# A planned two-block transformer kernel: searched issue order, later gate loads, constant rows on ScalarE

## Chip, cores, metric

One core of one Trainium2 chip. The metric is the device time of one execution in microseconds; the figure for a kernel is the median of its runs.

## What is computed

Two transformer blocks follow one another on x (32 x 128 x 256). The first is conditioned through shift, scale and gate vectors, which a product of the conditioning vector and `ada_w` gives; the second through scales and shifts of its normalisations.

```python
# first block
xm1 = _ln(x) * (1 + scale_sa) + shift_sa
x = x + gate_sa * (self_attention(xm1) @ sa_proj_w + sa_proj_b)
x = x + (cross_attention(_ln(x), context) @ ca_proj_w + ca_proj_b)
xm3 = _ln(x) * (1 + scale_ff) + shift_ff
x = x + gate_ff * (gelu(xm3 @ fc1_w + fc1_b) @ fc2_w + fc2_b)
# second block
x = x + rope_self_attention(_adaln(x, 1)) @ sa_out_w.T
x = x + rope_cross_attention(_adaln(x, 2), context) @ ca_out_w.T
x = x + gelu(_adaln(x, 3) @ ffn_w1.T + ffn_b1) @ ffn_w2.T + ffn_b2
```

All is float32, with 16 heads of 16 and a hidden width of 1024. Only the first block has gates: one row of 256 numbers for each batch entry and gate, multiplied into the output of a projection.

## The kernel before

The batch of 32 is cut into 16 groups of two (256 rows). Eight streams (`NS`) each carry one group through a block and then take the next. A group passes in the first block through normalisation, self-attention, normalisation, cross-attention, normalisation and feed-forward, then goes to memory (`middle`); later it comes back for the second block.

**The planner.** Each stream is a Python generator. Before every step it yields four things: when its inputs are ready, the engine, the kinds of buffer it needs, and a rank. `Clock` holds a model of the engines' free times and of the buffers (`clock.slots`), with a cost written beside each step (`clock.use("pe", 0.86 * n)`). `Tasks.run` takes for each engine the waiting task with the lowest lateness, rank and turn among those that could start within 0.02 us of the earliest, and then issues the engine whose choice starts first. The instructions are so issued in the planner's order; each engine, and the DMA queue of SP, works its own list in that order. What the model leaves out shows as a wait on the chip.

**Buffers.** There are one `scores` tile (four banks), one `small`, three `products` tiles in PSUM; five sets of `heads` (queries, keys, values, `top`); three `ou`; one pair of `ht` for feed-forward; and four `y` tiles. A `y` has two uses: `normed_T` writes normalised rows into it (L532), which TensorE transposes (L544), and `load_gate` loads gate rows into it from memory (L866), broadcast over 128 partitions, 256 KB.

**Attention** (from L695): for each half, scores (L708), their maxima on VectorE (`top`, L720), a transpose of those (L733), queries less maxima (`qa`, L737), scores again, the exponential on ScalarE (L746), the product with values (L754), and a copy to `ou` (L760). When both halves are copied, `over_sums` moves sums and rows by DMA: `few` (L772), `xt` (L774), a reciprocal (L777), `inv` (L780, L785), and the multiplication (L788) that the projection L821 waits for.

**The gates before.** `first_block` loads the self-attention gate right after the keys' product, before attention, and the stream loads the feed-forward gate before `fed_forward` starts. `project` multiplies gate and bias on GpSimd (L811), adds that to x (L812), multiplies the product in PSUM by the gate on VectorE (L830, into the gate's own tile) and adds it to x on GpSimd (L834), which frees the tile.

**Setting up.** `set_up` writes constant rows into queries and keys of each head set, on VectorE for the first (L338) and on GpSimd for the others in pieces of 256 (L335), then clears values and `top` (L341, L344). `the_rest` computes the modulations, gates and folded biases; `modulation`, `gated` and `with_values` put matrix products and the VectorE steps that read them into one planner's step.

Of the kernel before, what the change touches and what calls it, by code (L numbers as in the profile page):

```python
# [30 lines left out]
NEVER = 1e9  # L31


class Clock:


# [4 lines left out]
    def __init__(self):  # L41
        self.free = dict.fromkeys(("pe", "dve", "act", "pool", "sp", "none"), 0.0)
        many = {"sc": 1, "at": 1, "mm": 3, "pt": 2, "set": NA, "qa": 2, "ou": 3, "st": 2, "ht": 1,
                "y": 4, "cx": 3, "x": NS + 1}
        self.slots = {kind: [0.0] * n for kind, n in many.items()}
        self.table, self.way = None, "full"
        self.now = 0.0
        self.landed = 2.0
# [57 lines left out]
def when(t):  # L106
    return t() if callable(t) else t
# [6 lines left out]
class Tasks:  # L114


    def __init__(self, clock):
        self.clock = clock
        self.waiting = []

    def spawn(self, gen, owner):

        self.step([gen, None, owner])

    def step(self, task):
        task[1] = next(task[0], None)
# [3 lines left out]
    def run(self):  # L130
        clock = self.clock
        while self.waiting:

            first, chosen = {}, {}
            for task in self.waiting:
                ready, engine, kinds, rank = task[1]
                start, late = max(when(ready), clock.slot(kinds)), 0.0
                if engine in ("exp", "gelu"):
                    late = 0.0 if engine == clock.table else clock.TABLE
                    engine = "act"  # L140
                start = max(start, clock.free[engine])
                first.setdefault(engine, []).append((start, late, rank, task))
            for engine, l in first.items():
                horizon = min(start + late for start, late, _, _ in l)
                l = [(late, rank, task[2].turn(), start, i) for i, (start, late, rank, task) in enumerate(l)
                     if start + late <= horizon + 0.02]
                late, _, _, start, i = min(l)
                chosen[engine] = (start, first[engine][i][3])
            start, task = min(chosen.values(), key=lambda c: c[0])
            assert start < NEVER  # L150
            clock.now = start
            self.waiting.remove(task)
            self.step(task)
# [53 lines left out]
def two_blocks(ctx: ExitStack, tc: tile.TileContext, a: dict, out: bass.AP):  # L207
# [113 lines left out]

    clock.slots["set"] = [NEVER] * NA
    clock.use("pool", 1.5)
    clock.use("dve", 3.0)
    clock.use("act", 4.6)

    def set_up(i):
        hd = heads[i]
        for to, at in ((hd.q, None), (hd.k, 0)):
            src = rows[:, C:C + 1].to_broadcast([P, C]) if at is None else rows[:, 0:C]  # L330
            src = src.unsqueeze(2).to_broadcast([P, C, GT])
            if i:
                for c in range(C):
                    yield 2.5, "pool", "", 4
                    nc.gpsimd.tensor_copy(to[:, c, :], src[:, c, :])  # L335
                    clock.use("pool", 0.43)
            else:
                nc.vector.tensor_copy(to, src)  # L338
                clock.use("dve", 1.2)
        yield 0.0, "pool", "", 4  # L340
        nc.gpsimd.memset(hd.v, 1.0)  # L341
        clock.use("pool", 0.95)
        yield 0.0, "pool", "", 4
        nc.gpsimd.memset(hd.top, 0.0)  # L344
        clock.give("set", i, clock.use("pool", 0.2))

    r_sa, r_ca, r_fc2, r_f2 = [const.tile([P, D], F32, name=f"r_{name}") for name in ("sa", "ca", "fc2", "f2")]
    gbias = {"sa": spare[1][:B, 0:D], "ff": spare[1][:B, D:2 * D]}
# [78 lines left out]
    def landed(name):  # L427
        return lambda: there.get(name, NEVER)

    def modulation(name, w, emb, bias, wcol, bcol, one):  # L430

        slot, ps = mm([P, KC, B])
        t = const.tile([P, KC, B], F32, name=f"mod_{name}")
        for c in range(KC):
            at = wcol + c * P
            for k in range(KC):
                nc.tensor.matmul(
                    ps[:, c, :], lhsT=w[:, k, at:at + P], rhs=embT[emb][:, k, :],
                    start=(k == 0), stop=(k == KC - 1),
                )  # L440
        for c in range(KC):
            b = bias[:, bcol // P + c:bcol // P + c + 1]
            nc.vector.tensor_scalar(t[:, c, :], ps[:, c, :], b, 1.0 if one else 0.0, ALU.add, ALU.add)
        clock.use("pe", 1.0)
        clock.give("mm", slot, clock.use("dve", 0.5))
        return t

    mods, gates, biases = {}, {}, {"fc2": r_fc2, "f2": r_f2}

    def the_first():  # L450
        yield max(t_ada, 6.5), "pe", "mm", 0
        scale = modulation("sa_scale", ada_lo, "silu", c_ada, D, D, True)
        yield 0.0, "pe", "mm", 0
        mods["L0", "sa"] = scale, modulation("sa_shift", ada_lo, "silu", c_ada, 0, 0, False)

    def gated(name, w, wcol):

        slot, ps = mm([B, D])
        for k in range(KC):
            nc.tensor.matmul(ps, lhsT=embT["silu"][:, k, :], rhs=w[:, k, wcol:wcol + D],  # L460
                             start=(k == 0), stop=(k == KC - 1))
        t = gbias[name]
        nc.vector.tensor_tensor(t, ps, t, ALU.add)
        clock.use("pe", 0.9)
        clock.give("mm", slot, clock.use("dve", 0.5))
        gates[name] = dram.tile([B, D], F32, name=f"gate_dram_{name}")
        nc.sync.dma_start(out=gates[name], in_=t)
        clock.dma(2.0)

    def with_values(name, row, bias, w):  # L470

        wide = spare[0][:, 3 * D:4 * D].rearrange("p (k n) -> p k n", k=KC)
        slot, ps = mm([P, D])
        for k in range(KC):
            nc.vector.tensor_copy(wide[:, k, :], bias[:, k:k + 1].to_broadcast([P, P]))
            nc.tensor.matmul(ps, lhsT=wide[:, k, :], rhs=w[:, k, :], start=(k == 0), stop=(k == KC - 1))
        nc.vector.tensor_tensor(row, row, ps, ALU.add)
        clock.use("pe", 0.9)
        clock.give("mm", slot, clock.use("dve", 0.9))

    def the_rest():
        yield landed("gate_sa"), "pe", "mm", 1
        gated("sa", ada_lo, 2 * D)
        yield landed("w_sa"), "pe", "mm", 1
        with_values("sa", r_sa, c_qkv[:, 2 * KC:3 * KC], w_sa.t)
        biases["sa"] = r_sa
        yield landed("w_ca"), "pe", "mm", 1
        with_values("ca", r_ca, c_kv[:, KC:2 * KC], w_ca.t)
        biases["ca"] = r_ca
        yield landed("ff_shift"), "pe", "mm", 2  # L490
        shift = modulation("ff_shift", ada_lo, "silu", c_ada, 3 * D, 3 * D, False)
        yield landed("ada_hi"), "pe", "mm", 2
        mods["L0", "ff"] = (modulation("ff_scale", ada_hi, "silu", c_ada, 0, 4 * D, True), shift)
        yield landed("ada_hi"), "pe", "mm", 2
        gated("ff", ada_hi, D)
        load(lnw[2], "L1_xcond_ln3_w")
        there["ln3"] = clock.load(512)
        for i in (1, 2, 3):
            yield landed(f"ln{i}"), "pe", "mm", 2
            gamma = modulation(f"ln{i}_gamma", lnw[i - 1], "raw", c_ln[i - 1], 0, 0, True)  # L500
            yield landed(f"ln{i}"), "pe", "mm", 2
            mods["L1", i] = gamma, modulation(f"ln{i}_beta", lnw[i - 1], "raw", c_ln[i - 1], D, D, False)
            if i == 2:
                load(w_fc1.t, "L0_xcond_fc1_w")
                w_fc1.there[0] = clock.load(1024)
        load(w_fc2.t, "L0_xcond_fc2_w")
        w_fc2.there[0] = clock.load(1024)
        yield landed("ff_rows"), "none", "", 0
# [330 lines left out]
    def fed_forward(wm, x, t, w1, b1, w2, b2, gate, name):  # L839

        there = Event(FC)
        for f in range(FC):
# [9 lines left out]

            tasks.spawn(gelu(), wm)

        def lhs(k, b):
            return ht[k // (FC // 2)][:, k % (FC // 2), b * S:(b + 1) * S]

# [2 lines left out]
        return t  # L860

    def load_gate(wm, which, g):
        yield (lambda: 0.0 if which in gates else NEVER), "sp", "y", 2
        y = clock.take("y")
        t = ys[y]
        nc.sync.dma_start(out=t, in_=gates[which][g * GB:(g + 1) * GB, :].partition_broadcast(P))  # L866
# [22 lines left out]
    def attended(wm, at, x, masked, t, t_v, w, bias, gate, eps, mod, g, name, then, cx=None):  # L889
# [5 lines left out]
        if masked:  # L895
            end = yield from mask_row(heads[at], zeros, 0)
        clock.give("set", at, when(end))
        t = yield from project(wm, x, lambda k, b: wm.xt[:, k, b * S:(b + 1) * S], KC, w, done, bias, gate, name)
        return (yield from normed_T(wm, x, t, eps, mod, g, then))

# [15 lines left out]
    def first_block(wm, x, t, g):  # L916
# [1 line left out]
        at = yield from take_heads(wm, w_qkv, t)  # L918
        hd = heads[at]
        tk = yield from paired(hd, wm, w_qkv, wm.xt, t)  # L920
        gate = yield from load_gate(wm, "sa", g)
        tv = yield from values(wm, hd, w_qkv, 2 * D, wm.xt, t)
        cx = Context(g)
        t = yield from attended(wm, at, x, False, tk, tv, w_sa, "sa", gate, 1e-6, None, g, n, f"b{g}", cx)
        n = f"b{g}"
        at = yield from take_heads(wm, w_kv, latest(t, cx.there))
        hd = heads[at]
# [28 lines left out]
    def stream(wm, mine, loaded):  # L956

        while loaded:
# [3 lines left out]
                                    f"{'a' if first else 'd'}{g}")  # L962
            t = yield from (first_block if first else second_block)(wm, x, t, g)
            if first:
                gate = yield from load_gate(wm, "ff", g)
                to, args = middle, (w_fc1, c_fc1, w_fc2, "fc2", gate, f"c{g}")
            else:
                to, args = out, (w_fc1, c_f1, w_fc2, "f2", None, f"f{g}")

# [120 lines left out]
```

## Time and profile before

| | us |
|---|---|
| median of three runs | 1525.75 (1525.6 to 1532.34) |
| the profiled execution | 1528.39 |
| its span, first to last instruction | 1526.6 |
| VectorE busy in it | 899.8 |
| ScalarE busy in it | 690.2 |
| GpSimd busy in it | 371.0 |
| mean granted clock of TensorE | 0.985 |

The span leaves 1.8 us of the profiled execution's own time outside. In rows of the profile PE is TensorE's matmuls, PEld its weight loads, DVE VectorE, ACT ScalarE, POOL GpSimd, SP the engine whose queue issues the DMAs (SPq for its sequencer). L12 is line 12 of the kernel. A group's row reads: line, engine, operation, tile written and tiles read, shapes, count, busy time, mean ns of one, then the engine's idle time before such instructions and what ended it.

### The profile page before, as it was taken

The page shows a single profiled execution, that of the slowest core. Times are in us where ns is not written, and L with a number is a line of the kernel's source. Part 1 is how long each engine was busy: PE and PEld are TensorE (multiplying, and loading weights), DVE is VectorE, ACT ScalarE, POOL GpSimd, SP SyncE. Part 2 cuts the span into 40 slices and gives each one's busy share as a digit, 9 for nine tenths or more (in the row PEclk, how much of TensorE's full clock was granted, in tenths as well). Part 3 has the DMA queues.
Part 4 walks back from the last instruction along what each step waited for, and adds up shares of the span by engine and source line. Part 5 has one row for each costly group of instructions (what it writes and reads, how often), then busy time and mean ns, then how long its engine had stood idle before and what let it go on. Part 6 is the DMA issues. An engine that isn't in the chain of part 4 may idle for free.

```text
span 1526.6 us, 39576 instructions
## 1 busy us (share of the span) xinstructions
PE 1449.6 (95%) x16992; PEld 1193.1 (78%) x16992; DVE 899.8 (59%) x1544; ACT 690.2 (45%) x1110; POOL 371.0 (24%) x530
## 2 busy tenths in 40 slices
PE   6998799999999999998999999898999999999998
PEld 4776578888888877887777888776878878887887
DVE  5666555655546565555666564757595666577441
ACT  2443345554555444454534554443335535443541
POOL 6132221223221412334213322212121212222110
PEclk9999799999999999999999999999999999999999
DMA  6422124222222324121331431321131221212110
GB/s 212 143 68 78 60 69 106 70 62 82 80 65 69 89 79 123 54 83 52 91 107 63 132 98 43 95 68 62 53 108 47 76 77 55 95 53 87 33 50 21
DMA packets 107359, 120.50 MB, mean 79 GB/s; under 512 B 11632, under 2 KB 82992, under 8 KB 107184
## 3 DMA queue, kind: packets, MB, share of 16 engines
q1 hardware_dynamic: 107184, 117.98, 25.1%
q8 instruction: 133, 2.18, 0.6%
q14 instruction: 42, 0.34, 0.1%
HBM read 54.92 MB, written 12.68 MB: 44 GB/s over the span
## 4 chain that ended last, share of the span: by engine, by line
PE 77%; DVE 10%; DMA 6%; issue 3%; ACT 2%; SPq 1%; POOL 1%; DVEq 0%; ACTq 0%; POOLq 0%
PE products L583 25%; PE products L821 21%; PE scores L708 15%; PE small L754 6%; PE products L595 5%; DVE top L720 4%; PE products L544 3%; DVE y L532 1%; ACT exp L746 1%; PE small L733 1%; DMA ou<-inv_e 1%; DVE xt L788 1%; DMA ou<-inv_a 1%; DMA inv_a<-few_a 1%; DMA inv_e<-few_e 1%
## 5 line engine op out<-in xcount | busy, mean ns | idle before, releaser
L720 DVE TENSOR_REDUCE top<-scores 128x8 f32<-128x1024 f32 x256 | 300.0, 1213 | 70.2 <-PE scores L708 63.4
L746 ACT ACTIVATE exp<-scores 128x1024 f32<-128x1024 f32 x256 | 248.3, 1023 | 162.5 <-PE scores L708 158.2
L583 PE MATMUL products<-xt,w_ffn_w 128*128 128x256 f32 x1024 | 240.5, 388 | 1.1 <-ACT xt L562 0.9
L821 PE MATMUL products<-w_ffn_w,ht 128*128 128x256 f32 x1024 | 232.2, 382 | 0.0
L583 PEld LDWEIGHTS products<-xt,w_ffn_w 128*128 128x128 f32 x1024 | 191.3, 192 | 34.3 <-issue 2.8
L821 PEld LDWEIGHTS products<-w_ffn_w,ht 128*128 128x128 f32 x1024 | 191.7, 190 | 27.8
L708 PEld LDWEIGHTS scores<-qa,keys 32*128 32x128 f32 x4096 | 129.5, 191 | 66.7 <-issue 21.7
L760 ACT COPY ou<-small 128x512 f32<-128x512 f32 x128 | 75.5, 589 | 233.5 <-PE small L754 231.4
L708 PE MATMUL scores<-qa,keys 32*128 32x128 f32 x4096 | 154.3, 288 | 24.4 <-DVE top L720 12.0
L850 ACT ACTIVATE ht<-products,cols 128x256 f32<-128x256 f32 x256 | 116.5, 474 | 120.1 <-PE products L583 119.2
L708 PEld LDWEIGHTS scores<-keys,queries 32*128 32x128 f32 x4096 | 126.6, 187 | 37.1 <-issue 27.4
L708 PE MATMUL scores<-keys,queries 32*128 32x128 f32 x4096 | 151.2, 284 | 2.6 <-ACT exp L746 1.4
L688 POOL TENSOR_TENSOR st<-st 128x512 f32<-128x512 f32 x64 | 83.2, 1302 | 244.2 <-DVE st L683 224.6
L754 PE MATMUL small<-exp,values 128*32 128x128 f32 x4096 | 140.3, 278 | 1.8 <-ACT ou L760 1.4
L737 DVE TENSOR_TENSOR qa<-queries,small 128x512 f32<-128x512 f32 x128 | 86.3, 674 | 72.5 <-PE small L733 70.5
L583 PE MATMUL products<-xt,w_qkv_w 128*128 128x256 f32 x512 | 126.6, 393 | 1.0 <-ACT xt L562 0.9
L754 PEld LDWEIGHTS small<-exp,values 128*32 128x32 f32 x4096 | 105.3, 110 | 24.5 <-issue 10.1
L826 DVE TENSOR_TENSOR x<-products,x 128x512 f32<-128x512 f32 x64 | 44.1, 689 | 130.3 <-PE products L821 128.4
L788 DVE TENSOR_TENSOR xt<-xt,ou 128x512 f32<-128x512 f32 x64 | 52.7, 824 | 96.1 <-DMA ou<-inv_a 28.4
L583 PEld LDWEIGHTS products<-xt,w_qkv_w 128*128 128x128 f32 x512 | 95.5, 195 | 17.3 <-issue 2.8
L834 POOL TENSOR_TENSOR x<-y,x 128x512 f32<-128x512 f32 x32 | 40.7, 1273 | 277.9 <-DVE y L830 277.9
L603 ACT COPY values<-products 128x512 f32<-128x512 f32 x64 | 40.2, 628 | 132.1 <-PE products L595 129.7
(111 smaller groups left out, 1789.8 us busy)
## 6 DMA issues: line engine op xcount, KB each, us to landing
xt<-ou SPq DMA_DIRECT2D x64, 256.0 KB
keys<-st SPq DMA_DIRECT2D x96, 128.0 KB
queries<-st SPq DMA_DIRECT2D x96, 128.0 KB
cxt<-in_ctx SPq DMA_DIRECT2D x32, 256.0 KB
x<-in_x SPq DMA_DIRECT2D x16, 256.0 KB
y<-gate_dram_sa SPq DMA_DIRECT2D x16, 256.0 KB
keys<-st SPq DMA_DIRECT2D x16, 256.0 KB
ou<-inv_a SPq DMA_DIRECT2D x32, 128.0 KB
```

Of the source, the lines that this page charges most:

```text
L583: nc.tensor.matmul(ps[:, c, :], lhsT=w.t[:, k, at:at + P], rhs=src[:, k, :], start=(k == 0), stop=(k == KC - 1))
L595: nc.tensor.matmul(ps[:, b, :], lhsT=src[:, k, b * S:(b + 1) * S], rhs=w.t[:, k, col:col + D], start=(k == 0), stop=(k == KC - 1))
L688: nc.gpsimd.tensor_tensor(st[:, 0], st[:, 0], st[:, 1], ALU.add)
L708: nc.tensor.matmul(sc[:, r, c * S:(c + 1) * S], lhsT=lhs(slice(32 * r, 32 * r + 32), c), rhs=rhs(slice(32 * r, 32 * r + 32), c), start=Tru ...
L720: nc.vector.tensor_reduce(top[:, r:r + 2, TOP:TOP + 2 * C:2], scs[slot][:, r:r + 2, :].rearrange("p r (c s) -> p r c s", s=S), AX.X, ALU.max)
L737: nc.vector.tensor_tensor(qa, q[:, :, cut], ps.unsqueeze(1).to_broadcast([P, C, S]), ALU.subtract)
L746: nc.scalar.activation(exps[pt][r // 2], scs[slot][:, r:r + 2, :], AF.Exp, scale=SCALE)
L754: nc.tensor.matmul(ats[at][32 * r:32 * r + 32, c * S:(c + 1) * S], lhsT=v[:, b, i:i + HD, :].rearrange("p d t -> p (d t)"), rhs=exps[pt][r ...
L760: nc.scalar.copy(ous[ou[0]][:, :, cut], ats[at].rearrange("p (c s) -> p c s", s=S))
L788: nc.vector.tensor_tensor(wm.xt, wm.xt, by, ALU.mult)
L821: nc.tensor.matmul(ps[:, b, :], lhsT=lhs(k, b), rhs=w.t[:, k, :], start=(k == 0), stop=(k == n - 1))
L850: nc.scalar.activation(ht[f // (FC // 2)][:, f % (FC // 2), :], ps[:, 0, :], AF.Gelu, bias=b1[:, f:f + 1])
```

## The change

It has four parts.

1. A list of 36 numbers, one for each 40 us of the planner's time. Where a number is not zero, it changes the rank of about half the waiting tasks by a hash of the task's number, and sets how far behind the earliest start a task may lie and still be chosen.
2. Gate loads move: the one for self-attention from before attention to after its last product, directly ahead of `project`; the one for feed-forward from before the first hidden product to after the eighth. The planner counts, and the kernel has, three `y` tiles in place of four. A gate load waits in the planner until the gate's rows are in memory.
3. The constant rows of all five head sets are written by ScalarE in ten copies of 128x1024.
4. `modulation`, `gated` and `with_values` are split at the engines' borders; the bias copies of `with_values` come early and into a part of the tile for each; the loads that replace used weights wait for TensorE in the planner.

```diff
+EVERY = 40.0
+ORDER = (
+    200, 7, 0, 0, 0, 0, 297, 0, 0, 0, 0, 0, 0, 0, 0, 0, 129, 264, 0, 0, 0, 312, 0, 0, 0, 388, 0, 0, 109, 188, 182,
+    0, 0, 0, 292, 58
+)
...
-                "y": 4, "cx": 3, "x": NS + 1}
+                "y": 3, "cx": 3, "x": NS + 1}
...
+    def changed(self, task, rank, seed):
+        h = (task[3] * 40503 + seed * 2654435761 >> 4) * 2246822519 >> 11
+        return rank + (0, 0, 0, 0, -2, -1, 1, 2)[h % 8] if seed else rank
...
+            at = int(min(t for e, t in clock.free.items() if e in ("pe", "dve", "act")) / EVERY)
+            seed = ORDER[at] if at < len(ORDER) else 0
+            patience = (0.02, 0.02, 0.3, 0.8)[seed % 4]
...
-                l = [(late, rank, task[2].turn(), start, i) for i, (start, late, rank, task) in enumerate(l)
-                     if start + late <= horizon + 0.02]
+                l = [(late, self.changed(task, rank, seed), task[2].turn(), start, i) for i, (start, late, rank, task) in enumerate(l)
+                     if start + late <= horizon + patience]
...
     def set_up(i):
         hd = heads[i]
-        for to, at in ((hd.q, None), (hd.k, 0)):
...
         yield 0.0, "pool", "", 4
         nc.gpsimd.memset(hd.top, 0.0)
-        clock.give("set", i, clock.use("pool", 0.2))
+        end = clock.use("pool", 0.2)
+        for to, src in ((hd.q, rows[:, C:C + 1].to_broadcast([P, C])), (hd.k, rows[:, 0:C])):
+            yield 2.5, "act", "", 4
+            nc.scalar.copy(to, src.unsqueeze(2).to_broadcast([P, C, GT]))
+            end = max(end, clock.use("act", 1.02))
+        clock.give("set", i, end)
...
-    def modulation(name, w, emb, bias, wcol, bcol, one):
+    def modulation(ready, rank, name, w, emb, bias, wcol, bcol, one):
+        yield ready, "pe", "mm", rank
...
+        yield clock.use("pe", 1.0), "dve", "", 1
         for c in range(KC):
...
-    def with_values(name, row, bias, w):
-        wide = spare[0][:, 3 * D:4 * D].rearrange("p (k n) -> p k n", k=KC)
+    def with_values(ready, name, row, bias, w):
+        yield 8.0, "dve", "", 3
+        wide = spare[0][:, 3 * D:4 * D] if name == "sa" else spare[0][:, 2 * D:3 * D]
+        wide = wide.rearrange("p (k n) -> p k n", k=KC)
+        for k in range(KC):
+            nc.vector.tensor_copy(wide[:, k, :], bias[:, k:k + 1].to_broadcast([P, P]))
+        t = clock.use("dve", 0.4)
+        yield (lambda: max(t, ready())), "pe", "mm", 1
...
             if i == 2:
+                yield clock.free["pe"], "sp", "", 2
                 load(w_fc1.t, "L0_xcond_fc1_w")
...
+        if gate is not None:
+            gate = yield from load_gate(wm, "ff", gate)
...
     def load_gate(wm, which, g):
-        yield (lambda: 0.0 if which in gates else NEVER), "sp", "y", 2
+        yield (lambda: gates_at.get(which, NEVER)), "sp", "y", 2
...
         clock.give("set", at, when(end))
+        if gate is not None:
+            gate = yield from load_gate(wm, gate, g)
         t = yield from project(wm, x, lambda k, b: wm.xt[:, k, b * S:(b + 1) * S], KC, w, done, bias, gate, name)
...
         tk = yield from paired(hd, wm, w_qkv, wm.xt, t)
-        gate = yield from load_gate(wm, "sa", g)
...
-                gate = yield from load_gate(wm, "ff", g)
-                to, args = middle, (w_fc1, c_fc1, w_fc2, "fc2", gate, f"c{g}")
+                to, args = middle, (w_fc1, c_fc1, w_fc2, "fc2", g, f"c{g}")
```

More of the change, by code (lines that the diff above doesn't have):

```diff
@@ L119, in __init__ @@
         self.waiting = []
+        self.spawned = 0
     def spawn(self, gen, owner):
-        self.step([gen, None, owner])
+        self.spawned += 1
+        self.step([gen, None, owner, self.spawned])
+    def changed(self, task, rank, seed):
+        h = (task[3] * 40503 + seed * 2654435761 >> 4) * 2246822519 >> 11
+        return rank + (0, 0, 0, 0, -2, -1, 1, 2)[h % 8] if seed else rank
     def step(self, task):
@@ L323, in two_blocks @@
     clock.use("pool", 1.5)
-    clock.use("dve", 3.0)
-    clock.use("act", 4.6)
+    clock.use("dve", 3.9)
+    clock.use("act", 3.5)
     def set_up(i):
         hd = heads[i]
-        for to, at in ((hd.q, None), (hd.k, 0)):
[L330 to L339, printed above, removed]
         yield 0.0, "pool", "", 4
@@ L443, in modulation, with gated @@
             nc.vector.tensor_scalar(t[:, c, :], ps[:, c, :], b, 1.0 if one else 0.0, ALU.add, ALU.add)
-        clock.use("pe", 1.0)
         clock.give("mm", slot, clock.use("dve", 0.5))
         return t
-    mods, gates, biases = {}, {}, {"fc2": r_fc2, "f2": r_f2}
+    mods, gates, gates_at, biases = {}, {}, {}, {"fc2": r_fc2, "f2": r_f2}
     def the_first():
[L451 to L456, printed above, removed]
+        t = max(t_ada, 6.5)
+        scale = yield from modulation(t, 0, "sa_scale", ada_lo, "silu", c_ada, D, D, True)
+        shift = yield from modulation(t, 0, "sa_shift", ada_lo, "silu", c_ada, 0, 0, False)
+        mods["L0", "sa"] = scale, shift
+    def gated(ready, rank, name, w, wcol):
+        yield ready, "pe", "mm", rank
         slot, ps = mm([B, D])
@@ L461, in gated @@
                              start=(k == 0), stop=(k == KC - 1))
+        yield clock.use("pe", 0.9), "dve", "", 1
         t = gbias[name]
         nc.vector.tensor_tensor(t, ps, t, ALU.add)
-        clock.use("pe", 0.9)
-        clock.give("mm", slot, clock.use("dve", 0.5))
+        end = clock.use("dve", 0.5)
+        clock.give("mm", slot, end)
+        yield end, "sp", "", 1
         gates[name] = dram.tile([B, D], F32, name=f"gate_dram_{name}")
         nc.sync.dma_start(out=gates[name], in_=t)
-        clock.dma(2.0)
@@ L470, in with_values @@
-    def with_values(name, row, bias, w):
-        wide = spare[0][:, 3 * D:4 * D].rearrange("p (k n) -> p k n", k=KC)
+        gates_at[name] = clock.dma(2.0)
+    def with_values(ready, name, row, bias, w):
[6 more added lines that the diff above has]
+        yield (lambda: max(t, ready())), "pe", "mm", 1
@@ L473, in with_values @@
         slot, ps = mm([P, D])
         for k in range(KC):
-            nc.vector.tensor_copy(wide[:, k, :], bias[:, k:k + 1].to_broadcast([P, P]))
             nc.tensor.matmul(ps, lhsT=wide[:, k, :], rhs=w[:, k, :], start=(k == 0), stop=(k == KC - 1))
+        yield clock.use("pe", 0.9), "dve", "", 1
         nc.vector.tensor_tensor(row, row, ps, ALU.add)
-        clock.use("pe", 0.9)
-        clock.give("mm", slot, clock.use("dve", 0.9))
+        clock.give("mm", slot, clock.use("dve", 0.45))
@@ L481, in the_rest @@
+        biases[name] = row
     def the_rest():
[L482 to L495, printed above, removed]
+        yield from gated(landed("gate_sa"), 1, "sa", ada_lo, 2 * D)
+        yield from with_values(landed("w_sa"), "sa", r_sa, c_qkv[:, 2 * KC:3 * KC], w_sa.t)
+        yield from with_values(landed("w_ca"), "ca", r_ca, c_kv[:, KC:2 * KC], w_ca.t)
+        shift = yield from modulation(landed("ff_shift"), 2, "ff_shift", ada_lo, "silu", c_ada, 3 * D, 3 * D, False)
@@ L496, in the_rest @@
+        scale = yield from modulation(landed("ada_hi"), 2, "ff_scale", ada_hi, "silu", c_ada, 0, 4 * D, True)
+        mods["L0", "ff"] = scale, shift
+        yield from gated(landed("ada_hi"), 2, "ff", ada_hi, D)
+        yield clock.free["pe"], "sp", "", 2
         load(lnw[2], "L1_xcond_ln3_w")
@@ L498, in the_rest @@
         for i in (1, 2, 3):
[L499 to L502, printed above, removed]
+            gamma = yield from modulation(landed(f"ln{i}"), 2, f"ln{i}_gamma", lnw[i - 1], "raw", c_ln[i - 1], 0, 0, True)
+            beta = yield from modulation(landed(f"ln{i}"), 2, f"ln{i}_beta", lnw[i - 1], "raw", c_ln[i - 1], D, D, False)
+            mods["L1", i] = gamma, beta
             if i == 2:
+                yield clock.free["pe"], "sp", "", 2
                 load(w_fc1.t, "L0_xcond_fc1_w")
                 w_fc1.there[0] = clock.load(1024)
+        yield clock.free["pe"], "sp", "", 2
         load(w_fc2.t, "L0_xcond_fc2_w")
@@ L920, in first_block @@
         tk = yield from paired(hd, wm, w_qkv, wm.xt, t)
-        gate = yield from load_gate(wm, "sa", g)
         tv = yield from values(wm, hd, w_qkv, 2 * D, wm.xt, t)
         cx = Context(g)
-        t = yield from attended(wm, at, x, False, tk, tv, w_sa, "sa", gate, 1e-6, None, g, n, f"b{g}", cx)
+        t = yield from attended(wm, at, x, False, tk, tv, w_sa, "sa", "sa", 1e-6, None, g, n, f"b{g}", cx)
         n = f"b{g}"
```

## The prediction

> **What bounds the kernel now.** I read the page first, then a table of stretches, then what happens to one tile in the worst stretch.
>
> ```profile
> PE 1449.6 (95%) x16992; PEld 1193.1 (78%) x16992; DVE 899.8 (59%) x1544; ACT 690.2 (45%) x1110; POOL 371.0 (24%) x530
> ...
> PEclk9999799999999999999999999999999999999999
> ...
> PE 77%; DVE 10%; DMA 6%; issue 3%; ACT 2%; SPq 1%; POOL 1%; DVEq 0%; ACTq 0%; POOLq 0%
> ```
>
> TensorE is busy 95% of 1526.6 us and holds 77% of the chain that ended last. The change leaves its 16992 matmuls alone, so only 77.0 us of TensorE idle time and the time at a low clock (mean 0.985) can be won. Where they lie:
>
> ```profile
> 0.00:60.00 60.00, 43.86 (x387) 33.44 (x387) 38.82 (x101) 18.51 (x35) 28.63 (x70) 0.94 0.52 168
> 60.00:108.00 48.00, 46.60 (x569) 38.25 (x568) 30.60 (x53) 21.41 (x37) 13.00 (x18) 1.00 0.35 115
> 108.00:200.00 92.00, 74.10 (x1044) 59.19 (x1044) 48.04 (x70) 36.24 (x53) 17.78 (x25) 0.85 0.21 66
> 200.00:520.00 320.00, 318.25 (x3615) 263.73 (x3614) 180.47 (x317) 168.03 (x278) 84.64 (x123) 1.00 0.27 77
> 520.00:840.00 320.00, 303.53 (x3641) 250.13 (x3639) 192.06 (x324) 145.30 (x234) 92.82 (x125) 1.00 0.28 83
> ...
> 940.00:1120.00 180.00, 165.92 (x2174) 135.19 (x2173) 112.10 (x182) 75.16 (x114) 32.85 (x40) 0.97 0.21 67
> ```
>
> Columns: stretch, its length, busy time of PE, weight loads, DVE, ACT, POOL, granted clock, DMA share, GB/s. Idle PE: 16.1 us before 60, 17.9 in 108 to 200 (clock 0.85), 1.8 in 200 to 520, 16.5 in 520 to 840, 14.1 in 940 to 1120. In the third stretch PE does 74.10 x 0.85 = 63 us of full-clock work in 92: 29 us lost. In its middle one attention chain runs almost alone:
>
> ```profile
> 152.39 2.09 PE L708 MATMUL scores<-qa,keys 32*128 32x128 f32 x32 [2.48 <-DVE top L720]
> 154.41 0.47 PE L733 MATMUL small<-ident,top 128*128 128x128 f32 x1
> 156.59 2.09 PE L708 MATMUL scores<-qa,keys 32*128 32x128 f32 x32 [1.70 <-ACT exp L746]
> ```
>
> Why nothing else was at hand shows in the y tiles, between 95 and 182 us:
>
> ```profile
> L811 POOL TENSOR_TENSOR gb_a<-y,r_sa x8: 729/739/745, 97.9 to 179.6; 128x256 f32<-128x256 f32 x8
> L834 POOL TENSOR_TENSOR x<-y,x x4: 1262/1268/1275, 94.4 to 181.1; 128x512 f32<-128x512 f32 x4
> L866 SPq DMA_DIRECT2D y<-gate_dram_sa x3: 322/326/326, 95.7 to 140.2; - x3
> L830 DVE TENSOR_TENSOR y<-products,y x3: 655/682/691, 131.7 to 179.5; 128x512 f32<-128x512 f32 x3
> ```
>
> All four y tiles serve gates for 87 us: no L532 (normalised rows) and no L544 (their transposes) touches a y. The next normalisation stands at 182.86, and the streams whose projections had ended at 95.6, 133.7 and 140.2 start theirs from 201 on. The kernel starves itself by holding gates.
>
> **Gates behind attention.** 32 gates are held from their load (L866) to the end of L834. The ends sum to 1936 us more than the loads: 60.5 us each, 2.27 tiles of 4 on average until the last ends at 874.7. In the new place a self-attention gate is loaded at the end of attention. The chain from there to the end of L834 took 163.64 to 182.38 = 18.7 us once in the trace. A feed-forward gate is held for landing, what is left of the projection (32 matmuls, 6.91 us), L830 (0.69) and L834 (1.27): some 12. That is 16 x 18.7 + 16 x 12 = 491 us, 0.58 tiles, so three y tiles leave more free (2.4) than four did (1.7). A feed-forward stream that waits for a y now does so with the only ht in its hands, so the next feed-forward waits too; at 0.58 held I cost that at nothing, and without this slack it is the last rival's wait. What is late next is attention itself: it has one scores tile, used 256 times for a product of 1.17 and a reduction or exponential of 1.94 to 2.36, with hops about 3.8: 970 us of 1526, so it is no second wall, though it can bind locally. Bounds for 108 to 200: nothing, or all 29 us. Other streams are ready there, yet the stretch also lacks feed-forward work, whose first product stands at 186.26; I take two thirds: **-19**. 520 to 840 is still the block with gates, and PE waits there are spread over scores, xt and y: bounds 0 and -16.5, I take half, **-8**.
>
> Here a rule can be weighed. The granted clock was 0.50 from 155 to 160 us, while no PE gap between 145 and 200 was over 2.48 us. The Trainium skill (TensorE: Matmul & The Clock Gate, Why this matters for your kernels) asks for no idle gap above about 3 us if the clock is to hold; the trace differs, since here shorter gaps in a row did it. By that rule the 11 us that the low clock cost in 108 to 200 would not come back with the gaps, and the sum would be -24 in place of -31.
>
> **The searched order.** 12 of 36 numbers are not zero. A number changes the ranks of about half the tasks (by -2 to 2) and the patience (0.02, 0.3 or 0.8) in 40 us of the planner's time. Nothing is computed differently; instructions change places on their engines. No row prices this. From both sides: 940 to 1120 lost 14.1 idle and 180 x 0.03 = 5.4 of clock, together at most -19; a foreign order that makes this stretch as poor as 108 to 200 would cost as much. One number (388) covers 1000 to 1040; the planner sees no gate landing and no SP queue, so much of what it gains on paper can be lost: **-5**. The three numbers for 1120 to 1240 lie where only 4.5 us idle are left until the end of the span.
>
> **Constant rows on ScalarE.** POOL drops 32 copies (6.5 + 5.8 = 12.3 us, rows L335), DVE two (0.95 + 0.88). ScalarE gets ten of 128x1024: between 0.95 (DVE's) and 1.18 (twice the 0.589 of a 128x512 ACT copy); near the 1.02 of a 128x1024 exponential, so 10.2 us. ScalarE idled 11.10 us until 14.56, which covers them; without it the first xt is one copy, 1.0 us, late. POOL's last set-up memset (34.1 us) comes to about 7 (five pairs of 0.95 + 0.2 from 1.4), so head sets come free earlier. DVE's bias copies ahead of L476 leave their PE wait (1.45) and the split of modulation lets the first statistics pass the second modulation's wait (1.29 on DVE), part of the 3.19 PE gap at 13.21. Bounds 0 and -9.7 (16.1 less the first load's 6.43): **-3**. Later loads of weights wait in the planner instead of blocking SP (some 29 us of SP waits at L244, none ending a PE wait): 0; PE gets 0 from it whatever SP does next.
>
> **What the gates cost in their new place.** L811 and L812 follow the load at once, so POOL stands until the gate lands, and ve, rstd and st of other streams stand behind it. Before, seven feed-forward gates did so already (32.2 us, up to 7.2); their landing took 3.5 to 4.4 us after issue (185.43 to 188.94, 450.40 to 454.80), and the 40-us stretches with two of them (240 to 280, 440 to 480) show PE busy 40.00 of 40. So nothing on PE from that. On SP the feed-forward load moves past the next x load (256 KB, L301), which no row shows PE waiting for after the start. For self-attention, the 256 KB come ahead of few and xt on SP: the chain few, inv, ou, L788 (about 10 us) gets longer. I take a third of 3.9 = 1.3 us, bounds 0 and 3.9; 16 chains; PE waits of 14.6 us in 12 cases already end at L788, so I let a fifth through: 16 x 1.3 x 0.2 = **+4** (bounds 0 and 62).
>
> **Sum:** -19 - 8 - 5 - 3 + 4 = -31. The profiled execution took 1528.39 (span 1526.6 and 1.8 around it), giving 1497; the median 1525.75 lies 2.6 lower: **1495 us**.
>
> **Rivals.**
> - *A fuller mend.* 29 + 16.5 + 19.5 + 9.7 lost us could come back; four fifths of these 75 are 60: 1466. For it: 200 to 520 runs with 1.8 us idle, so the mix can fill PE. Against: the first feed-forward product cannot come at once. 0.13.
> - *The clock stays low though gaps close.* The rule above; two thirds of 17.9 is 12 in place of 19: 1502. Against: the clock row. 0.05.
> - *It doesn't free anything.* Three tiles instead of four, with waiting streams taking them in the same crowd, plus an order made for another clock: 1525. Against: 0.58 tiles held. 0.11.
> - *Slower: the feed-forward gate is late.* Its cover is the projection, 6.91 us; landing and four POOL instructions (2 x 0.77 + 2 x 0.73) take 3.5 to 4.4 + 3.0 = 6.5 to 7.4. Nothing is left over. SP serves in order, and one L866 wait was 11.24 us (at 331.68). Every us that SP is late keeps L830 at DVE's head, with top reductions and qa behind it, for which PE waits. From 31 / 16 = 1.9 us a gate the gain is gone; at 3 us, 48 is lost: 1495 + 48 = 1543. For it: DVE already waited 29.5 us at L830 with no cause shown. Against: SP's waits at L866 sum to about 42 us over 32 gates, 1.3 each. 0.17.
>
> **How the numbers follow.** The forecast gets 0.54, its own range 1480 to 1512. About 0.5% (1518.1 to 1533.4) is what a measurement here can tell from no change. Faster is 0.54 + 0.13 + 0.05 = 0.72, same 0.11, slower 0.17. The range runs from the fuller mend to the edge of the slower case, 1463 to 1532; about 0.05 lies below, 0.14 above.
>
> **What would show it.** Right: between 95 and 200 us L532 and L544 use y, the clock is above 0.95, PE idles under 8 us there; the first L583 of feed-forward stands before 186; L335 and L338 are gone and ten ACT copies end before 15 us. POOL's wait for gates grows from 32 us to over 60, with no more PE waits for L788 than 15 to 20 us. Wrong: the hole of 108 to 200 stands again, or DVE waits at L830 grow beyond 100 us with PE idle behind top.

## The result and the profile after

The changed kernel took 1486.8 us (median, 1485.06 to 1490.8) against 1525.89 us for the kernel before beside it: a ratio of 0.9738, 95% interval 0.9705 to 0.977. The profiled execution took 1490.8 us, its span 1488.7. From the page of the changed kernel, the rows that answer to those shown before:

```profile
PE 1441.7 (97%) x16992; PEld 1187.0 (80%) x16992; DVE 876.8 (59%) x1514; ACT 711.0 (48%) x1150; POOL 359.9 (24%) x498
...
PEclk9999999999999999999999999999999999999999
...
PE 80%; DMA 7%; DVE 6%; SPq 2%; issue 2%; ACT 2%; POOL 1%; DVEq 0%; ACTq 0%; POOLq 0%
```

TensorE's idle time fell from 77.0 to 47.0 us (span less busy time), and its busy time by 7.9 us at the same count of matmuls, because the mean clock rose from 0.985 to 0.992 (busy time times clock is 1428 us before and 1430 after). The same stretches as before, with the same columns:

```profile
0.00:60.00 60.00, 51.65 (x508) 43.45 (x508) 44.14 (x110) 34.29 (x61) 13.60 (x34) 1.00 0.53 176
60.00:108.00 48.00, 45.90 (x677) 36.80 (x666) 27.89 (x44) 24.23 (x37) 14.29 (x19) 1.00 0.42 120
108.00:200.00 92.00, 85.39 (x1112) 69.47 (x1111) 53.34 (x92) 44.99 (x74) 22.59 (x34) 0.96 0.27 77
200.00:520.00 320.00, 314.79 (x3693) 260.76 (x3694) 174.03 (x302) 167.47 (x280) 91.49 (x131) 0.99 0.26 77
520.00:840.00 320.00, 310.74 (x3764) 254.21 (x3763) 195.06 (x332) 151.50 (x241) 89.69 (x119) 0.99 0.29 87
...
940.00:1120.00 180.00, 176.66 (x2104) 145.02 (x2105) 115.22 (x194) 81.03 (x131) 37.96 (x48) 0.99 0.22 70
```

Every poor stretch is better: idle time went from 16.1 to 8.4 us before 60, from 17.9 to 6.6 in 108 to 200, from 16.5 to 9.3 in 520 to 840, from 14.1 to 3.3 in 940 to 1120. The good one, 200 to 520, idles 3.4 us more than before. In the y tiles between 95 and 182 us the normalisations (L547, the old L532) are back, and only two gates are loaded for self-attention:

```profile
L547 DVE TENSOR_SCALAR y<-x,mv_b,rstd_b x8: 407/409/817, 102.9 to 163.2; 128x256 f32<-128x256 f32 x8
...
L884 SPq DMA_DIRECT2D y<-gate_dram_sa x2: 437/448/460, 114.0 to 149.2; - x2
```

So far this looks like the forecast. The experiments say that the forecast's steps are not why the kernel got faster.

### The profile page after: what moved, and what is told of

It is laid out like the page before. It is cut to its first block, busy times and chain, and to the rows that moved or that the text cites. A ratio compares the mean times of both kernels' runs of the same rounds, so it can differ in the third digit from the quotient of the medians.

```text
span 1488.7 us, 39505 instructions
## 1 busy us (share of the span) xinstructions
PE 1441.7 (97%) x16992; PEld 1187.0 (80%) x16992; DVE 876.8 (59%) x1514; ACT 711.0 (48%) x1150; POOL 359.9 (24%) x498
## 4 chain that ended last, share of the span: by engine, by line
PE 80%; DMA 7%; DVE 6%; SPq 2%; issue 2%; ACT 2%; POOL 1%; DVEq 0%; ACTq 0%; POOLq 0%
PE products L598 26%; PE products L836 22%; PE scores L723 15%; PE small L769 7%; PE products L610 6%; PE products L559 3%; DVE top L735 2%; DMA ou<-inv_a 1%; PE small L748 1%; ACT exp L761 1%; DVE xt L803 1%; DMA ou<-inv_d 1%; DMA ou<-inv_b 1%; PE products L448 1%; DVE y L547 1%
## 5 line engine op out<-in xcount | busy, mean ns | idle before, releaser
L803 DVE TENSOR_TENSOR xt<-xt,ou 128x512 f32<-128x512 f32 x64 | 48.8, 762 | 93.9 <-DMA ou<-inv_a 32.5
L698 DVE TENSOR_TENSOR st<-products,rope 128x512 f32<-128x512 f32 x128 | 81.5, 684 | 13.7 <-PE products L598 9.7
L845 DVE TENSOR_TENSOR y<-products,y 128x512 f32<-128x512 f32 x32 | 22.1, 689 | 108.4 <-PE products L836 92.8
```

What stands on the lines that cost most here:

```text
L698: nc.vector.tensor_tensor(st[:, :, :, one], ps[:, :, one].unsqueeze(2).to_broadcast([P, 2, 2, S]), rope, ALU.mult)
```

## Experiments

Ratios are to the kernel before on the same chip, with 95% intervals. A change of 0.0066 in a ratio is 10 us.

**Taking the change apart.** First, all 36 numbers set to zero.

```diff
-ORDER = (
-    200, 7, 0, 0, 0, 0, 297, 0, 0, 0, 0, 0, 0, 0, 0, 0, 129, 264, 0, 0, 0, 312, 0, 0, 0, 388, 0, 0, 109, 188, 182,
-    0, 0, 0, 292, 58
-)
+ORDER = (0, 0, 0, 0, 0, 0, 0, 0, 0, 0, 0, 0, 0, 0, 0, 0, 0, 0, 0, 0, 0, 0, 0, 0, 0, 0, 0, 0, 0, 0, 0, 0, 0, 0, 0, 0)
```

> The changed kernel with all 36 numbers zero, all else kept. My theory (the list is worth about 5 us, the rest comes from the gates and the start): 1492, between 1487 and 1500. Rival (the list carries most of the 39 us gained): 1510 or more, with the hole between 108 and 200 us back.

Measured: 1522.72 us, 0.9987 (0.9971 to 1.0003). My theory falls: without the list no gain is left that could be told from none. The rival holds in its total, but not in its picture, as the stretches of this kernel show:

```profile
60.00:108.00 48.00, 42.06 (x590) 34.10 (x583) 24.61 (x45) 18.41 (x29) 12.15 (x17) 0.93 0.35 115
108.00:200.00 92.00, 82.17 (x1095) 66.18 (x1094) 54.40 (x88) 41.28 (x65) 20.66 (x31) 0.98 0.29 81
200.00:520.00 320.00, 307.80 (x3623) 253.46 (x3622) 176.45 (x309) 162.40 (x269) 86.46 (x124) 0.99 0.24 73
520.00:840.00 320.00, 304.33 (x3559) 251.42 (x3558) 175.88 (x307) 151.69 (x244) 90.72 (x124) 0.99 0.29 87
...
1120.00:1480.00 360.00, 345.50 (x4010) 285.70 (x4003) 194.60 (x315) 168.93 (x271) 62.12 (x82) 0.98 0.19 60
```

The hole of 108 to 200 is mended without the list: 82.17 us busy at 0.98 is 81 us of full-clock work, 18 more than the 63 of the kernel before. The gain is given back elsewhere: 60 to 108 idles 5.9 us where it idled 1.4, 200 to 520 idles 12.2 where it idled 1.8, 1120 to 1480 idles 14.5 where it idled 4.3.

Next, the two gate loads alone, with three y tiles.

```diff
-                "y": 4, "cx": 3, "x": NS + 1}
+                "y": 3, "cx": 3, "x": NS + 1}
...
+        if gate is not None:
+            gate = yield from load_gate(wm, "ff", gate)
...
         clock.give("set", at, when(end))
+        if gate is not None:
+            gate = yield from load_gate(wm, gate, g)
...
-        gate = yield from load_gate(wm, "sa", g)
...
-                gate = yield from load_gate(wm, "ff", g)
```

> The kernel before with only the two gate loads moved behind attention and behind the eighth hidden product, and three y tiles. My theory (-19 in 108 to 200, -8 in 520 to 840, +4): about 1503, with L532 using y between 95 and 182 us. Rival (the place of the loads changes nothing, the stretch lacks work for another reason): 1526 and the same hole.

Measured: 1532.0 us, 1.0048 (1.003 to 1.0065), so slower. The first part of my theory holds in the y tiles of this kernel (normalisations in the hole), the second does not: the chain of one attention stands there all the same.

```profile
L532 DVE TENSOR_SCALAR y<-x,mv_b,rstd_b x5: 405/407/1371, 94.8 to 140.9; 128x256 f32<-128x256 f32 x5
```

```profile
149.46 1.17 PE L708 MATMUL scores<-keys,queries 32*128 32x128 f32 x32
153.12 2.09 PE L708 MATMUL scores<-qa,keys 32*128 32x128 f32 x32 [2.48 <-DVE top L720]
155.14 0.47 PE L733 MATMUL small<-ident,top 128*128 128x128 f32 x1
157.31 2.09 PE L708 MATMUL scores<-qa,keys 32*128 32x128 f32 x32 [1.70 <-ACT exp L746]
...
186.42 1.23 PE L544 MATMUL products<-ident,y 128*128 128x128 f32 x4 [3.86 <-DVE y L532]
```

TensorE's order of time shows the serial pattern again: scores, a wait for the maxima, a transpose, scores, a wait for the exponential. y tiles are free and streams have normalised, so y was one wait of several. What TensorE waits for here are the maxima and exponentials of the one scores tile. Nine sets of values were written by 137.0 us and eleven halves of attention copied to `ou` by 148.8, so three or four attentions stood ready for that tile. The two streams that had normalised at 132 and 140 got no product before 170. No run had a second scores tile. The last row leads to a second finding. GpSimd, just before it:

```profile
181.80 0.74 POOL L811 TENSOR_TENSOR gb_a<-y,r_sa 128x256 f32<-128x256 f32 x1 [11.56 <-DMA y<-gate_dram_sa]
182.62 0.72 POOL L812 TENSOR_TENSOR x<-x,gb_a 128x256 f32<-128x256 f32 x1
183.30 0.72 POOL L811 TENSOR_TENSOR gb_a<-y,r_sa 128x256 f32<-128x256 f32 x1
184.10 0.72 POOL L812 TENSOR_TENSOR x<-x,gb_a 128x256 f32<-128x256 f32 x1
184.90 0.22 POOL L524 TENSOR_SCALAR ve_c<-mv_c 128x2 f32<-128x2 f32 x1
```

GpSimd stood for a gate until 181.80 and worked on it for 3 us; the `ve` of another stream, whose statistics VectorE had finished by 180.23, stood behind it until 184.90. VectorE then waited 5.72 us at its normalisation (L532) for rstd, and TensorE 3.86 us. Moving the gates made GpSimd's waits for gates grow from 32.2 us to 230.2 here, and to 256.5 in the changed kernel.

Then a fifth y tile with the old gates (`"y": 5`).

> The kernel before with five y tiles in place of four, gates where they were. If starvation of y is the cause, a fifth tile lets at least one stream normalise in the hole: 1508 to 1520. Rival (the gain of late gates comes from the order on SP and POOL, not from free tiles): 1526 within 4 us.

Measured: 1528.19 us, 1.002 (1.0001 to 1.0038). More y tiles bring nothing, although three streams now normalise between 96 and 142 us (rows of L532). The stretch of 108 to 200 did get better (79.58 us busy at 0.93 in place of 74.10 at 0.85), and the rest gave it back. Then only the constant rows (`set_up` as in the change). Part 4 was not run by itself.

> The kernel before with only the constant rows moved to ScalarE. My theory: 1 to 3 us from a start less hindered, 1523. Rival (early head sets are what fills the first stages): 1514 or less, with the hole between 108 and 200 gone too.

Measured: 1549.87 us, 1.0168 (1.0137 to 1.0199): 26 us slower. The start, for which it was meant, improved a little, and the hole of 108 to 200 much:

```profile
0.00:60.00 60.00, 47.05 (x374) 37.80 (x378) 37.10 (x100) 29.39 (x53) 16.31 (x38) 0.91 0.59 195
...
108.00:200.00 92.00, 81.44 (x1199) 64.97 (x1192) 55.34 (x83) 40.77 (x64) 23.06 (x31) 0.96 0.28 82
...
1120.00:1480.00 360.00, 338.90 (x3786) 280.74 (x3785) 190.41 (x319) 158.96 (x255) 60.61 (x81) 0.98 0.18 57
```

In the hole that is 81.44 x 0.96 = 78 us of full-clock work, with the gates where they were: more than with late gates alone (66, from 75.94 at 0.87) and nearly the 81 of the change without its list. From 1120 to 1480 TensorE idles 21.1 us, where the kernel before idled 4.3, and after 1480 another 25.0, before 4.1. The groups end badly spread, a thousand microseconds after the edit: the last group's rows leave at 1544 us, 55 us after those of the group before it, in the kernel before 14 us. Each edit moves every later choice of the planner; what an edit does in its own stretch says little about the end.

**How the list works.** Only its first two numbers kept:

```diff
-    200, 7, 0, 0, 0, 0, 297, ...
...
+ORDER = (200, 7, 0, 0, 0, 0, 0, ...)
```

> The changed kernel with only the first two of its twelve numbers (200 and 7, the first 80 us of the planner's time), the other ten zero. Theory A (a list works through its end result: where the order of the first 80 us leaves the streams decides the waits of the whole run): 1495 to 1505, over half of the 36 us between the list and no list, though only 80 of 1500 us are touched. Theory B (each number mends the 40 us that it stands for): about 1516, an even share of the gain.

Measured: 1491.99 us, 0.9748 (0.9724 to 0.9771). Theory A holds, more strongly than expected: two numbers for the first 80 us bring 0.0239 of the 0.0249 between no list and the whole list; the other ten bring too little to tell from nothing here. From 80 us on, both kernels plan by the same rules, yet compare with the rows of the kernel without a list:

```profile
60.00:108.00 48.00, 45.97 (x672) 37.23 (x669) 28.30 (x45) 24.24 (x37) 14.34 (x19) 1.00 0.41 119
108.00:200.00 92.00, 85.59 (x1112) 69.58 (x1111) 52.42 (x91) 45.76 (x74) 22.59 (x33) 0.96 0.27 77
200.00:520.00 320.00, 313.42 (x3689) 259.68 (x3688) 174.42 (x301) 166.98 (x278) 91.24 (x131) 0.99 0.26 77
520.00:840.00 320.00, 312.38 (x3704) 257.71 (x3703) 189.18 (x322) 154.57 (x249) 90.89 (x122) 0.99 0.31 92
```

Busy time is 3.9, 3.4, 5.6 and 8.1 us higher. The first hidden product of feed-forward stands at 163.7 us, against 185.0 without a list, so one group is ahead of the rest earlier; but that alone is not the gain, as the next two kernels show. Why these two numbers do that, and others not, the trace does not tell.

To see whether any shuffling would do, 12 was added to each of the twelve numbers; the places and the patience stay.

```diff
-    200, 7, 0, 0, 0, 0, 297, ...
...
+ORDER = (212, 19, 0, 0, 0, 0, 309, ...)
```

> The changed kernel with 12 added to each of the twelve numbers, so that the places and the patience stay and other tasks are moved. Theory S (the list is a choice among many orders, and an unchosen one is no better than none): 1520 to 1545. Rival (more patience and some shuffling in these places are what helps): within 10 us of 1487.

Measured: 1533.19 us, 1.0026 (1.001 to 1.0043). The list is worth something only because it was chosen. Feed-forward starts early here too, at 167.0 us. Then the kernel before, with the machinery of the list and a list searched for it:

```diff
+ORDER = (2168, 0, 0, 0, 0, 0, 0, 1062, 0, 0, 2143, 0, 0, 2508, 881, ...)
...
     many = {"sc": 1, "at": 1, "mm": 3, "pt": 2, "set": NA, "qa": 2, "ou": 3, "st": 2, "ht": 1,
             "y": 4, "cx": 3, "x": NS + 1}
```

> The kernel before (four y tiles, early gates, constant rows on GpSimd and VectorE) with only the machinery of the list and a list of its own, found by the same kind of search. Theory S (the search makes the gain, on the old structure too): 1490 to 1502. Rival (late gates and early head sets are needed for a list to find anything): 1515 or more.

Measured: 1494.52 us, 0.9771 (0.9751 to 0.9791). With early gates, four y tiles and slow constant rows, a searched list brings 2.3% by itself, with feed-forward starting as late as 216.0 us. The two lists were not searched equally long, so the 0.3% between this kernel and the changed one cannot be put down to the gates.

**The price of the gates' new place.** The four GpSimd instructions on a gate are issued later, after the products of the projection's first half (self-attention) or second half (feed-forward); the order on all other engines stays, and so does the planner's account. The traces show the same instructions in the same order on TensorE, VectorE and ScalarE, so this comparison is free of the planner's turns. Without a list:

```diff
+        def beside():
+            for b in range(GB):
+                gb = p_s.tile([P, D], F32, tag="gb", name=f"gb_{name}_{b}", bufs=2)
+                nc.gpsimd.tensor_tensor(gb, gate[:, b, :], bias, ALU.mult)
+                nc.gpsimd.tensor_tensor(x[:, b, :], x[:, b, :], gb, ALU.add)
...
-                    gb = p_s.tile([P, D], F32, tag="gb", name=f"gb_{name}_{b}", bufs=2)
-                    nc.gpsimd.tensor_tensor(gb, gate[:, b, :], bias, ALU.mult)
-                    nc.gpsimd.tensor_tensor(x[:, b, :], x[:, b, :], gb, ALU.add)
...
             t = clock.use("pe", 0.43 * n)
+            if gate is not None and b == int(n > KC):
+                beside()
```

> The changed kernel without a list, and the four GpSimd instructions on a gate (L826, L827 in the changed kernel) issued after the first half of the projection (self-attention) or the second (feed-forward), by when the gate has landed; the order on every other engine is the same. If GpSimd's waits for gates delay rstd, y and TensorE (15.4 us of TensorE waits on y without a list, 9 us of it where rstd came late): 1510 to 1516, against 1522 for the kernel without a list. Rival (those waits are hidden): 1520 to 1525; or slower, if VectorE now waits for GpSimd at the gate's multiplication.

Measured: 1513.18 us, 0.9889 (0.9861 to 0.9916) against 0.9987 without this edit: 1.0%, 15 us. TensorE's waits at the transposes of y, first without the edit, then with it:

```profile
PE products L556 <- DVE y L544: 15.4, 11, 4.9
```

```profile
PE products L556 <- DVE y L544: 3.6, 5, 1.4
```

They fell by 11.8 us. VectorE paid little for it: its idle time at the gate's multiplication is 115.6 us against 111.3, and 4.6 of it now waits for GpSimd. I had expected each gate to have landed by then, but GpSimd still waits 114.6 us for gates, against 217.6; so the 15 us are what this later place gives back, not the whole price. With the list of the change:

> The changed kernel with its own list, and the GpSimd instructions on a gate issued later as in e8; the order on every other engine is that of the changed kernel. Theory (GpSimd's wait for a gate costs what TensorE waits on y where rstd came late: here 6.1 us in all, 4 of it from late rstd): 1481 to 1485 against 1486.8. Rival (nothing left to gain, since the list already avoids these places): 1486 to 1488.

Measured: 1480.73 us, 0.9683 (0.966 to 0.9706), 0.0055 below the changed kernel, 8 us. The total is as the theory had it, with a little more gained, but the way is another. TensorE's waits on y fell from 6.0 to 2.3 us, yet between the two profiled executions its idle time fell only from 47.0 to 46.0 us. Its busy time fell from 1441.7 to 1432.5, because the clock rose from 0.992 (0.995 in the changed kernel's three other executions) to 0.999. On the kernel with late gates alone:

> The kernel of e2 (only late gates, no list) with the GpSimd instructions on a gate issued later. TensorE waited 17.6 us on y in e2, 5 of it at the start. Theory: 1532 falls by 8 to 12 us to 1520 to 1524, so that late gates alone are no longer a loss. Rival (late gates lose by the order that they bring): 1529 to 1533.

Measured: 1529.13 us, 0.9994 (0.9972 to 1.0016) against 1.0048: 0.0054, 8 us. In the ratio the theory holds, and late gates alone are no loss any more; the median, which I had named, does not show it, since the kernel before ran at 1529.32 us on that chip.

**Searching further.** Once with a planner that knows the wait: GpSimd's gate work is charged after the gate's landing, and the list is searched anew.

```diff
+            clock.free["pool"] = max(clock.free["pool"], gate_at)
...
+            return clock.use("pool", 2.9)
...
-        yield t, "dve", "", 1
+        yield max(t, gated), "dve", "", 1
...
-        clock.dma(3.6)
+        clock.gate_at = clock.dma(4.0)
```

> As e9, with the planner charging GpSimd's gate work where it now stands and after the gate's landing, and a list searched anew for this planner. Theory (a planner that knows this wait can be searched as far as the old one, and loses less on the chip): 1478 to 1486. Rival (the new list ends on other waits that the planner does not know): 1488 to 1498.

Measured: 1468.26 us, 0.9607 (0.9579 to 0.9634), the fastest of all and below the range that I gave.

```profile
PE 1428.0 (98%) x16992; PEld 1178.8 (80%) x16992; DVE 876.8 (60%) x1514; ACT 713.0 (49%) x1152; POOL 357.3 (24%) x498
```

TensorE idles 36.5 us of 1464.5. Once with the change's own planner and its list searched further:

> As e9, with the list of the change searched further on the old planner (nine of its numbers changed or added). Theory (the gain of the search comes through nearly whole): 2 to 4 us below e9. Rival (what is gained so late is the planner's own error): within 3 us of e9 or above it.

Measured: 1473.29 us, 0.9634 (0.9608 to 0.9659): 0.0049 below e9, 7 us, where 2 to 4 were expected. What is found late in the search still comes through on the chip. Whether the fastest kernel owes its further 5 us to what its planner knows or to its other list is open, since both changed at once.

## Why the prediction was right, and where its steps were wrong

The total was right: -31 us forecast, -39 measured, 1495 against 1486.8, inside the forecast's own range. The terms were not, so that the total came out is luck: -27 us were put on the gates and -5 on the list, and it was the list that brought the 38.

- **What bounds the kernel.** Right: only TensorE's idle and low-clock time was won (77.0 to 47.0 us idle, 7.9 us of busy time).
- **Gates behind attention, -19 and -8.** Wrong in kind. The gates are held for 20.3 us each (60.5 before; I had 15.3), and y is free in the hole. But late gates alone cost 0.5%, a fifth y tile brought nothing, and constant rows alone mended more of the hole than late gates did (78 us of full-clock work against 66). The step that failed is "All four y tiles serve gates for 87 us" with its "The kernel starves itself by holding gates": the trace showed that no stream could get a y, not that a stream with a y would have had work for TensorE. With y free, in the kernel of late gates, three or four attentions stood ready for the one scores tile, which I had set aside as no second wall.
- **Adding stretches.** The hole did gain what I forecast (82 us of full-clock work after, 63 before, so the -19 came true as a number), but without the list the same 18 us there left the whole at 0.9987. A gain in one stretch of a planned order is no term of a sum while every later choice moves with it.
- **The searched order, -5.** Mis-sized: 0.0249, 38 us. I priced each number by the idle time of the 40 us that it names; two numbers for the first 80 us moved waits 600 us and more later. My doubt that much of the planner's gain would be lost on the chip was not borne out: lists found on the planner's clock gained 2.3 to 2.5% here.
- **Constant rows, -3.** The direct part was right: ten ACT copies of 1.04 us (1.02 forecast), the last done at 12.9 us, idle time before 60 us halved in the changed kernel. Alone, the rows took that idle time from 16.1 to 13.0; part 4, which was not run alone, or the order made the rest. In the total, the edit alone cost 26 us through the order at the end.
- **The gates' new place, +4.** Mis-sized and on another path. "So nothing on PE from that" was wrong: seven waits with a busy TensorE were too few to conclude from; with 29 at least 8 us can be won back (15 without the list). Without the list it went by way of rstd and y, with the list mostly by the clock. The path that I priced, the `ou` chain, shows no such cost: TensorE's waits for L803 are 10.5 us, 14.6 before.
- **The slower rival.** VectorE's idle time at the gate's multiplication went from 103.4 to 108.4 us; nothing of it. The sign named for it, over 100 us, could not have told: the kernel before stood above it.
- **The clock rule.** By the rule weighed there (the Trainium skill, TensorE: Matmul & The Clock Gate, Why this matters for your kernels), the 11 us of low clock in the hole were not tied to its gaps. The clock there rose from 0.85 to 0.96 as the gaps went, so the trace stays against the rule. What lowers the clock here stands in the last section.
- **Signs named beforehand.** Right: feed-forward starts before 186 (164.4), L335 and L338 are gone, between 95 and 200 us TensorE idles 7.4 us at a clock of 0.97, GpSimd's waits for gates passed 60 us, TensorE's for L803 did not grow. None of them told the theories apart; taking out the list did.

Open is what late gates are worth on their own: orders that were not chosen lie between 0.9987 and 1.0168 (e1, e2, e3, e4, e6, e11), more apart than the effect, and no two structures were searched equally long.

## What to carry to other kernels

Where a greedy planner fixes the order of a nearly full engine, one edit reshuffles everything after it: unchosen orders here spread over 1.8% of the time, and a search among them was worth 2.3 to 2.5%, more than the edits around it. Test such edits with the order held fixed (as in e8 and e9), or search each version equally long; a single order of each shows luck. And before pricing a freed buffer, ask what the stream that gets it would wait for next; before moving a load close to its use, ask which in-order engine will stand at the head of its queue for it, and whose work is behind.

## What was not expected of the hardware

Short gaps were enough to lower TensorE's clock, and where a gap lies counts as much as how long it is. In each trace the granted clock is either 1.00 or 0.50, and it changes only at the borders of a grid of 3.41 us. Stretches of this grid in the changed kernel, with the columns of the stretches above:

```profile
126.46:129.87 3.41, 1.61 (x35) 1.12 (x33) 0.69 (x1) 2.56 (x3) 0.00 (x0) 1.00 0.32 106
129.87:133.28 3.41, 2.35 (x8) 1.55 (x12) 0.69 (x1) 0.00 (x0) 0.00 (x0) 0.50 0.24 57
133.28:136.70 3.42, 3.42 (x36) 2.60 (x32) 0.00 (x0) 1.58 (x2) 0.00 (x0) 0.50 0.02 5
136.70:140.11 3.41, 3.41 (x50) 2.58 (x53) 1.61 (x4) 1.12 (x3) 2.25 (x3) 1.00 0.06 14
...
413.17:416.59 3.42, 2.20 (x17) 1.52 (x13) 1.08 (x2) 3.15 (x4) 0.00 (x0) 1.00 0.67 201
416.59:420.00 3.41, 3.06 (x68) 2.69 (x69) 0.21 (x1) 1.94 (x5) 2.15 (x3) 1.00 0.12 36
...
573.61:577.02 3.41, 1.50 (x15) 1.04 (x8) 2.39 (x4) 2.14 (x3) 2.33 (x5) 1.00 0.24 53
577.02:580.43 3.41, 3.41 (x19) 2.35 (x22) 2.02 (x5) 1.85 (x5) 0.00 (x0) 0.50 0.06 19
580.43:583.85 3.42, 3.42 (x68) 2.87 (x64) 0.00 (x0) 2.48 (x4) 0.00 (x0) 1.00 0.77 215
```

A gap of 2.86 us that ends at 130.93 left its stretch busy for 1.61 us, and two stretches at half clock followed. A gap of 1.55 us that ends at 575.58 left 1.50, and one followed. A gap of 1.57 us that ends at 416.94 lies across a border: its stretch was busy for 2.20, and the clock stayed.

The 14 traces together, from the first change of clock to the last matmul: after a stretch at full clock in which TensorE, by the trace's modelled ends, was busy for under 45%, the next was at half clock in all 57 cases; over 53%, in 4 of 5853; between, in 24 of 42. After a stretch at half clock, the next was at half again in all 43 cases under 83%, and in 2 of 87 above; none lay between 83 and 85%. Executions of one kernel differ in it: on the last chip the kernel before took from 1523.98 us at a mean clock of 0.988 to 1536.74 at 0.980.

So in these kernels a gap that takes more than some half of one such stretch also costs the next stretch half its clock, an estimated 1.7 us; after that, only a nearly full stretch brings the clock back. This is why fewer gaps also made TensorE's busy time shorter. In the fastest kernel no gap after the start is above 1.84 us, and its clock is 1.00 until its last matmul.
